# A four-layer cross-attention network in one core: norms loaded by broadcast, and the order of loads, tokens, divisions and stores changed at a dozen places

## The chip, the cores and the metric

The kernel runs on one core of one Trainium2 chip. Its time is the device time of one execution in microseconds (us). Three executions of the kernel before gave 1397.26, 1397.42 and 1398.39 us; the median, 1397.42, stands for it. The profile is of a further execution, which took 1396.16 us.

The core has five engines with queues of their own: TensorE (PE; the load of its stationary operand is shown as PEld), VectorE (DVE), ScalarE (ACT), GpSimd (POOL) and SyncE (SP, which here only issues DMAs).

## The reference

All numbers are float32. `x` has 4 batches of 256 tokens of 256 elements; `ctx` has 4 batches of 512 rows of 128. Four times a layer norm, a cross-attention and a residual sum follow each other, and then a layer norm, a feed-forward block and a residual sum:

```
# attention 0: 16 heads of 16; q and k are normed per head; the last 16 rows of
# ctx have their own k, v, norm weights and softmax, whose result is added
q = ln(x @ Wq + bq, qn); k = ln(y_main @ Wk + bk, kn); k_dca = ln(y_dca @ Wkv_dca + b, knd)
ctx = attn(q, k, v) + attn(q, k_dca, v_dca);  return ctx @ Wo + bo
# feed-forward 0: of 64 low-rank maps the 4 with the longest A x are taken
# attentions 1, 2, 3: 16 heads of 128, 8 key heads, mask, no bias
scores = (x @ Wq) (ctx @ Wk)^T / sqrt(128);  return softmax(scores) (ctx @ Wv) @ Wo
# feed-forward 1: 8 experts, 2 for each token, and a shared expert
# feed-forward 2: the one of 2 experts (gelu or relu) that a gate prefers
# feed-forward 3: the 64 tokens of each batch that a router scores highest
```

## The kernel before

The function that runs (`bounded_path`) holds one long program whose order is written out by hand for PE, ACT, DVE and POOL; each engine works through its own instructions in that order and waits on semaphores of others. A second path for inputs outside some bounds lies behind a branch and does not run. All is in tiles of 128 partitions; a batch of `x` is one tile `x_sb[b]` of 128 x 2 x 256, where partition p holds tokens 2p and 2p+1.

**Opening and layer 0** (to about 222 us). `Norm(b)` (L908 on) computes mean and reciprocal deviation of a batch, its `tokens` the normed tokens `xn`, and `layernorm_T` (L932) turns them into `xnT` by PE. The opening fills PE with matmuls nobody reads (`warm`, L1428). Weights are centred per head on DVE (`centred`, L1146). The norms' weights and biases, three loads `prm` of one partition each (L1061), are copied out on POOL into `rep`, and eight matmuls of one column (`pcols`) turn them into per-partition columns `cols`, which scale the turned queries and keys. `project_q`, `project_k`, `project_v` make queries, keys and values; class `Scale` makes the heads' reciprocal deviations in steps: `square` on ACT, `sum` on DVE, `power` on ACT, `root` (three DVE operations, L1247 to L1249) and `scaled` (L1252), whose result `pad` PE turns (`pT`, L1329) into qT (L1336) and kT (L1347, L1352). Scores are `ps` (L1361), the attended values `po` (L1371). In the loop over steps of batch b, the norm and the tokens of a later batch are placed at fixed steps i. Feed-forward 0 (`ysf`, L1497; added to x on POOL, L1498) ends with the tokens of layer 1's first batch.

PSUM: until the end of layer 0 banks come from a pool `ring`; then it is closed and a pool `psum` opened (L1750).

**Layers 1 to 3** (`attention`, L1777). Beforehand the query and key weights of a head are multiplied into one matrix (`folding`, L975: `pm` L986 into `m_sb`, `pn` L1002 into `n_sb`) from raw weights that `load_raw` (L958) brings from HBM, 1280 KB for each of four parts. Then come, for each of 32 pairs of a batch and two heads, queries, scores (`ps`, L1905), their exponential, and `po` (L1913). Sums are inverted and spread (`wide`, L1959, a DVE transpose), and the attended values are divided by a multiply of 128 x 512 (`divided`, L1960), on POOL and DVE in turn. The last four pairs are divided at the layer's end; `last_output` (`py`, L1995) then multiplies them by `n_sb`, first for token chunk 0, then 1, and `out.add` adds the other pairs' part `w` to x.

**Feed-forward 1** (552 to 655 us): lists of tokens by expert, indirect DMAs on POOL that fetch a block's tokens (`gather`, L2398), `turn_in` (pxg, L2406, and its copy xgT, L2408), expert matmuls (pgu, L2431) and the shared expert (`psh`, `pysh`, L2270).

**Feed-forward 2** (to about 1035 us): 9 blocks `blocks2`, of which blocks 0 to 4 hold the first three batches' tokens, and 5 to 8 the rest. Each has `gather` (L2795), `turn_in` (pxg, L2803; xgT, L2805), `weights` (a DVE copy `wa`, L2819, and an ACT copy `wb`), `rise2` (pb, L2833; z, L2838), `either` and `fall` (pyb, L2859; yb, L2863; a store `yd` on SP, L2864). Layer 3's four raw loads are issued on SP after the stores of blocks 0, 1, 4 and 5.

**Feed-forward 3** (to the end): `put` (L3235 to L3248) adds the routed tokens' part to x and stores a batch; batches 2 and 3 are computed in two column halves and stored whole, both by DMAs on ACT's queue.

```
for k in range(4):
    divided(B - 1, 4 + k, nc.vector if k % 2 else nc.gpsimd)     # layer's end
out.add()
...
(nc.scalar if i else nc.sync).dma_start(out[b]..., x_sb[b])      # put
```

## Time and profile before

| | us |
|---|---|
| median of three executions | 1397.42 |
| the profiled execution | 1396.16 |
| its span, first to last instruction | 1394.3 |
| outside the span | 1.86 |
| PE busy | 1377.1 |
| DVE busy | 887.7 |
| POOL busy | 682.8 |
| ACT busy | 580.3 |
| mean granted TensorE clock | 0.999 |

The page of the profile gives each engine's busy time with its share of the span and, as x and a number, its instructions; then the chain of work that ended last, followed back from the end, with its shares by engine; then groups of instructions by source line. The waits view lists, for one engine, who ended its idle times: the waiting tile and line, the releasing engine and tile, then us in all, the number of times and the longest. A timeline line gives start, length, engine, line, operation, output and inputs, shapes, and in brackets the idle time before it and who ended it. SPq and ACTq are DMAs as SP and ACT issue them: the time is that of the issue, not of the transfer. A matmul of float32 shows as two PE instructions (and PE's lines here name the number of these).

### The profile page before, as it was taken

The page shows a single profiled execution, that of the slowest core. Times are in us where ns is not written, and L with a number is a line of the kernel's source. Part 1 is how long each engine was busy: PE and PEld are TensorE (multiplying, and loading weights), DVE is VectorE, ACT ScalarE, POOL GpSimd, SP SyncE. Part 2 cuts the span into 40 slices and gives each one's busy share as a digit, 9 for nine tenths or more (in the row PEclk, how much of TensorE's full clock was granted, in tenths as well). Part 3 has the DMA queues.
Part 4 walks back from the last instruction along what each step waited for, and adds up shares of the span by engine and source line. Part 5 has one row for each costly group of instructions (what it writes and reads, how often), then busy time and mean ns, then how long its engine had stood idle before and what let it go on. Part 6 is the DMA issues. An engine that isn't in the chain of part 4 may idle for free.

```text
span 1394.3 us, 19995 instructions
## 1 busy us (share of the span) xinstructions
PE 1377.1 (99%) x7279; PEld 907.2 (65%) x7279; DVE 887.7 (64%) x2018; ACT 580.3 (42%) x1148; POOL 682.8 (49%) x822
## 2 busy tenths in 40 slices
PE   9999999999999999999999999999999999999998
PEld 7665676566656666887565666666875656666666
DVE  6667863665666547655576756549656758566675
ACT  5766454433344332256434333333264344333331
POOL 4223333466565455232577654566315775445560
PEclk9999999999999999999999999999999999999999
DMA  5000220300000001172110000000422000000000
GB/s 167 2 1 2 76 77 16 79 21 1 8 0 8 1 8 36 44 236 67 38 54 8 16 1 9 0 0 16 148 88 65 9 4 4 0 1 0 1 0 34
DMA packets 49622, 47.05 MB, mean 34 GB/s; under 512 B 8297, under 2 KB 45386, under 8 KB 49516
## 3 DMA queue, kind: packets, MB, share of 16 engines
q1 hardware_dynamic: 45868, 37.43, 8.9%
q0 software_dynamic: 2544, 6.95, 1.7%
q8 instruction: 60, 0.98, 0.3%
q10 hardware_dynamic: 1104, 1.31, 0.3%
q14 instruction: 46, 0.38, 0.1%
HBM read 38.73 MB, written 6.95 MB: 33 GB/s over the span
## 4 chain that ended last, share of the span: by engine, by line
PE 94%; DVE 2%; POOL 2%; DMA 1%; issue 1%; ACT 0%; SPq 0%; DVEq 0%; POOLq 0%
PE ps L1905 23%; PE po L1913 23%; PE paq L1875 6%; PE pao L1875 5%; PE pbq L1875 4%; PE pbo L1875 3%; PE ps L1361 2%; PE pyf L1495 2%; PE paf L1445 2%; PE pgu L2431 2%; PE po L1371 2%; PE psh L2253 1%; PE pm L986 1%; PE pn L1002 1%; PE py L1995 1%; PE pyb L2859 1%
## 5 line engine op out<-in xcount | busy, mean ns | idle before, releaser
L1924 POOL TENSOR_TENSOR half<-pT 128x1024 f32<-128x1024 f32 x93 | 218.4, 2348 | 288.9 <-ACT pT L1908 216.6
L1905 PE MATMUL ps<-qT,cT 128*128 128x512 f32 x768 | 345.6, 593 | 0.0
L1913 PE MATMUL po<-pT,c_sb 128*128 128x512 f32 x768 | 345.3, 592 | 0.0
L1908 ACT ACTIVATE pT<-ps,mbias 128x512 f32<-128x512 f32 x384 | 263.7, 687 | 155.4 <-PE ps L1905 139.8
L1913 PEld LDWEIGHTS po<-pT,c_sb 128*128 128x128 f32 x768 | 145.8, 190 | 183.2 <-issue 183.2
L1905 PEld LDWEIGHTS ps<-qT,cT 128*128 128x128 f32 x768 | 138.9, 190 | 138.4 <-issue 136.1
L1917 ACT COPY oT<-po 128x512 f32<-128x512 f32 x96 | 56.2, 586 | 265.2 <-PE po L1913 265.2
L1960 POOL TENSOR_TENSOR oT<-oT,wide 128x512 f32<-128x512 f32 x90 | 114.4, 1290 | 16.8 <-DVE wide L1959 16.8
L1885 DVE TENSOR_TENSOR qT<-qT,paq 128x128 f32<-128x128 f32 x90 | 25.5, 283 | 96.3 <-ACT qT L1884 96.3
L1365 ACT ACTIVATE pT<-ps 128x512 f32<-128x512 f32 x128 | 66.0, 602 | 26.5 <-PE ps L1361 26.2
L1932 DVE TENSOR_TENSOR half<-half 128x512 f32<-128x512 f32 x96 | 71.9, 749 | 2.7 <-POOL half L1922 2.5
L1934 DVE STREAM_TRANSPOSE turned<-half 128x512 f32<-128x512 f32 x96 | 68.3, 712 | 6.3
L1885 DVE TENSOR_TENSOR w<-w,pao 128x128 f32<-128x128 f32 x21 | 6.0, 286 | 103.0 <-ACT w L1884 103.0
L1875 PE MATMUL paq<-xnT_a,m_sb 128*128 128x128 f32 x360 | 71.3, 280 | 0.0
L1875 PE MATMUL paq<-xx,m_x 128*128 128x128 f32 x360 | 69.6, 275 | 0.0
L1875 PEld LDWEIGHTS paq<-xnT_a,m_sb 128*128 128x128 f32 x360 | 57.2, 192 | 16.7 <-issue 8.5
L1938 DVE TENSOR_REDUCE sums<-turned 128x16 f32<-128x512 f32 x96 | 65.8, 686 | 3.3
L1875 PE MATMUL pao<-n_x,ox 128*128 128x128 f32 x336 | 65.0, 275 | 0.0
L1884 ACT COPY qT<-paq 128x128 f32<-128x128 f32 x90 | 23.9, 265 | 94.1 <-PE paq L1875 94.1
L1959 DVE STREAM_TRANSPOSE wide<-rz 128x512 f32<-128x512 f32 x96 | 62.2, 686 | 0.1
L1888 DVE TENSOR_TENSOR qT<-qT,pbq 128x384 f32<-128x384 f32 x90 | 49.9, 554 | 9.7 <-DVE qT L1887 0.5
L1875 PEld LDWEIGHTS paq<-xx,m_x 128*128 128x128 f32 x360 | 54.7, 192 | 0.0
(484 smaller groups left out, 2530.2 us busy)
## 6 DMA issues: line engine op xcount, KB each, us to landing
wq<-in_L_wqT SPq DMA_DIRECT2D x11, 512.0 KB
wo<-in_L_wo SPq DMA_DIRECT2D x11, 512.0 KB
yd<-yr SPq DMA_DIRECT2D x20, 128.0 KB
xd<-xn_f SPq DMA_DIRECT2D x8, 256.0 KB
w<-in_F_w SPq DMA_DIRECT2D x4, 512.0 KB
wk<-in_L_wkT SPq DMA_DIRECT2D x11, 128.0 KB
wv<-in_L_wvT SPq DMA_DIRECT2D x11, 128.0 KB
yd<-yb SPq DMA_DIRECT2D x9, 128.0 KB
```

The source lines that it names most:

```text
L1365: nc.scalar.activation(pT[kp][:, j], ps[j], AF.Exp)
L1875: nc.tensor.matmul(p[:, at, :], lhsT=lhsT, rhs=rhs, start=(k == 0 and at == 0), stop=(k == len(of) - 1 and i == which[-1]),)
L1905: nc.tensor.matmul(ps, lhsT=cT[:, b, k * P : (k + 1) * P], rhs=qT, start=True, stop=True)
L1908: nc.scalar.activation(pT[:, k, :], ps, AF.Exp, bias=mbias[:, b, k : k + 1])
L1913: nc.tensor.matmul(po, lhsT=c_sb[:, b, k, :], rhs=pT[:, k], start=(k == 0), stop=(k == NK - 1))
L1917: done["head"] = nc.scalar.copy(raw, po).ins
L1924: nc.gpsimd.tensor_tensor(half, pT[:, 0:2], pT[:, 2:4], ALU.add)
L1932: nc.vector.tensor_tensor(part, half[:, 0], half[:, 1], ALU.add)
L1934: nc.vector.transpose(turned.rearrange("p f i -> p (f i)"), part)
L1938: nc.vector.tensor_reduce(sums[b, hp // 4][:, hp % 4, :], turned, AX.X, ALU.add)
L1959: nc.vector.transpose(wide, rzs[b, hp // 4][:, hp % 4, :, None].to_broadcast([P, NB, 32]))
L1960: eng.tensor_tensor(outs[b, hp], outs[b, hp], wide.rearrange("p f i -> p (f i)"), ALU.mult)
```

## The change

- Norms: `prm` is loaded onto all 128 partitions; on each, the elements of its own lane are picked by a product with `lane0` (made from the identity) and a sum. The copies `rep` on POOL and the eight `pcols` matmuls are gone; `columns_of_norms` moves ahead of add_q. One `warm` group is 3 in place of 4; the first queries go ahead of the biases on PE; the centring of `wq0` goes ahead of that of the bias rows; the first heads' `root` is made by four POOL operations; ACT's copies of the values of batch 0 for the last rows come after qT and kT.
- In batch 1 of layer 0 the norm of batch 3 and its tokens are placed one step later; the tokens of layer 1's first batch go before the last output step of feed-forward 0.
- The pool of banks is changed after layer 1's first queries.
- The last division of layers 1 to 3 is done by halves (128 x 256): first the four first halves (for token chunk 0), then the second.
- Feed-forward 1: block 0's `turn_in` goes ahead of the second `pysh` of batch 2; the first `pysh` of batch 3 goes ahead of `pm`.
- Feed-forward 2: raw loads 1, 2, 3 of layer 3 are issued after the stores of blocks 4, 5 and 6 (before: 1, 4 and 5); block 6's weights are copied before block 4's `fall`.
- The stores of batches 2 and 3 go by column halves, batch 3's on SP and batch 2's on ACT.

The diff, cut to its core (line numbers of before in the headers):

```diff
@@ 1052 @@ opening: loads, lanes, columns
-        rep = w0.tile([1, 8, 4, 2, HD0], F32, tag="qT0", name="rep")
-        prm = l0.tile([1, 3, 2, HD0], F32, tag="prm", name="prm")
+        prm = l0.tile([P, 3, 2, HD0], F32, tag="prm", name="prm")
...
-            nc.sync.dma_start(prm[:, i], t[f"L0_{n}"].rearrange("(o a) x -> o a x", o=1))
+            nc.sync.dma_start(prm[:, i], t[f"L0_{n}"].partition_broadcast(P))
...
-        nc.vector.memset(rep, 0.0)
+        nc.vector.tensor_reduce(
+            lane0.rearrange("p o x -> p (o x)"), ident.rearrange("p (a q) -> p q a", q=2 * HD0), AX.X, ALU.add
+        )
+        nc.vector.tensor_reduce(halves0, lane0, AX.X, ALU.add)
+        nc.vector.tensor_tensor(lane0[:, 0], lane0[:, 0], lane0[:, 1], ALU.add)
...
+            def root_aside(self, a, z):
+                v, r, e = (t[:, a:z] for t in (self.v, self.r, self.e))
+                nc.gpsimd.tensor_tensor(e, r, r, ALU.mult)
+                nc.gpsimd.tensor_tensor(e, e, v, ALU.mult)
+                nc.gpsimd.tensor_scalar(e, e, -0.5, 1.5, ALU.mult, ALU.add)
+                nc.gpsimd.tensor_tensor(r, r, e, ALU.mult)
...
         def columns_of_norms():
-            pn = state0.pop()
-            c_v = cols.rearrange("p i a -> p (i a)")
-            nc.vector.tensor_scalar(c_v[:, :4], pn[:, :4], HD0 ** -0.5, None, ALU.mult)
-            nc.vector.tensor_copy(c_v[:, 4:], pn[:, 4:])
+            nc.vector.tensor_tensor(by_lane, prm, lane0[:, 0, None, None, :].to_broadcast(wide), ALU.mult)
+            nc.vector.tensor_reduce(pairs, by_lane, AX.X, ALU.add)
+            for o in range(2):
+                nc.vector.tensor_scalar(
+                    cols[:, o, :], pairs[:, 0, :], halves0[:, o : o + 1], HD0 ** -0.5, ALU.mult, ALU.mult
+                )
+            nc.vector.tensor_copy(cols[:, 2:, :], pairs[:, 1:, :])
@@ 1509 @@ opening: order
+        centred(by_head(wq0), by_head(wq0), mq)
         centred(by_head(crow), by_head(crow), head_sums(by_head(crow), 3), 3)
-        centred(by_head(wq0), by_head(wq0), mq)
...
-        warm(4)
+        columns_of_norms()
+        warm(3)
+        add_q = project_q(0)
         spread_biases()
-        add_q = project_q(0)
         add_q()
...
-        context_T(1)
-        norm_columns()
         sc0.sum(0, NC)
...
         sc0.square(True, NC + 2, NQK)
+        context_T(1)
         sc0.sum(NC, NC + 2)
+        ones_of_values()
+        sc0.root_aside(0, NC)
+        last_context(1)
...
-        sc0.root(0, NC)
         sc0.scaled(0, NC)
@@ 1615 @@ layer 0
-                if i == 5:
+                if i == (5 if n == 1 else 6):
                     norms[n + 1] = Norm(n + 1, f"a0_{n + 1}")
-                elif i == 6:
+                elif i == (6 if n == 1 else 7):
                     xns[n + 1] = norms[n + 1].tokens()
...
+                if n == 6:
+                    xn1 = norm.tokens()
                 if n:
                     arrows[n].output()
@@ 1751, 2008 @@ pool of banks
-    del banks["ring"]
-    banks["psum"] = ctx.enter_context(tc.tile_pool(name="psum", bufs=2, space=PSUM))
...
             first_queries(0)
+            if "ring" in banks:
+                del banks["ring"]
+                ring.close()
+                banks["psum"] = ctx.enter_context(tc.tile_pool(name="psum", bufs=2, space=PSUM))
@@ 2054 @@ layers' ends
+            widths = []
+            for k in range(0, 4, 2):
...
+                for j in range(2):
...
+                    nc.vector.transpose(wide, rzs[B - 1, 1][:, k + j, :, None].to_broadcast([P, NB, 32]))
...
+                divided_half(k, widths[k], 0, nc.gpsimd)
+                divided_half(k + 1, widths[k + 1], 0, nc.vector)
             for k in range(4):
-                divided(B - 1, 4 + k, nc.vector if k % 2 else nc.gpsimd)
+                divided_half(k, widths[k], 1, nc.vector if k % 2 else nc.gpsimd)
             out.add()
@@ 2524, 2563 @@ feed-forward 1
+            blocks[0].turn_in()
             shared[2].down(1)
             shared[2].add(1)
-            for j in range(-2, NBLK + 1):
+            for j in range(-1, NBLK + 1):
...
+            shared[3].down(0)
             for n in range(N8):
                 next(fold)
                 if n < NC:
-                    shared[3].down(n)
+                    if n:
+                        shared[3].down(n)
@@ 2976 @@ feed-forward 2
-            load_raw(3, 1, done["slots2"])
...
             blocks2[6].turn_in()
+            blocks2[6].weights(fp)
             blocks2[4].fall(fp)
-            load_raw(3, 2, done["slots2"])
+            load_raw(3, 1, done["slots2"])
...
                     rise2(5)
-                    blocks2[6].weights(fp)
...
                 blocks2[i].fall(fp)
+                if i in (5, 6):
+                    load_raw(3, i - 3, done["slots2"])
                 if i == 5:
-                    load_raw(3, 3, done["slots2"])
@@ 3248 @@ stores
-                (nc.scalar if i else nc.sync).dma_start(out[b].rearrange("(p c) d -> p c d", c=NC), x_sb[b])
+                (nc.scalar if i and not b % 2 else nc.sync).dma_start(
+                    out[b].rearrange("(p c) d -> p c d", c=NC)[:, :, cols], x_sb[b][:, :, cols]
+                )
...
-        put(1, cols=a, store=False)
+        put(1, cols=a)
```

More of the change, by code (lines that the diff above doesn't have):

```diff
@@ L848, in bounded_path @@
     w0 = first.enter_context(tc.tile_pool(name="w0", bufs=2, side="right"))
-    banks = {"ring": first.enter_context(tc.tile_pool(name="ring", bufs=6, space=PSUM))}
+    ring = ctx.enter_context(ExitStack())
+    banks = {"ring": ring.enter_context(tc.tile_pool(name="ring", bufs=6, space=PSUM))}
     def bank(tag, shape, name):
@@ L1103, in bounded_path @@
         nc.gpsimd.memset(c_last, 0.0)
-        nc.vector.memset(rep, 0.0)
+        lane0 = l0.tile([P, 2, HD0], F32, tag="lane0", name="lane0")
+        halves0 = l0.tile([P, 2], F32, tag="halves0", name="halves0")
+        nc.vector.tensor_reduce(
[3 more added lines that the diff above has]
+        nc.vector.tensor_tensor(lane0[:, 0], lane0[:, 0], lane0[:, 1], ALU.add)
         rows = l0.tile([P, 2], F32, tag="rows", name="rows")
@@ L1201, in project_k, with project_v @@
             return lambda: nc.vector.tensor_tensor(qks[b][:, NC + k0 : NC + k0 + 2, :], pk, bias, ALU.add)
-        def project_v(b):
+        def project_v(b, later=None):
             for k0 in range(0, NK + 1, 2):
@@ L1209, in project_v, with kept @@
                     nc.tensor.matmul(pv[:, k - k0], lhsT=ck, rhs=wvo[:, int(k == NK)], start=True, stop=True)
-                for o, (h, _) in enumerate(halves):
-                    if k0 < NK:
-                        nc.scalar.copy(vals[b % 2][:, k0 : k0 + 2, o, :, h], pv[:, :, o])
-                    else:
-                        nc.scalar.copy(vals_d[b % 2][:, o, :, h], pv[:, 0, o])
+                def kept(k0=k0, pv=pv):
+                    for o, (h, _) in enumerate(halves):
+                        if k0 < NK:
+                            nc.scalar.copy(vals[b % 2][:, k0 : k0 + 2, o, :, h], pv[:, :, o])
+                        else:
+                            nc.scalar.copy(vals_d[b % 2][:, o, :, h], pv[:, 0, o])
+                if later is None:
+                    kept()
+                else:
+                    later.append(kept)
         class Scale:
@@ L1258, in bounded_path, with columns_of_norms @@
         cols = l0.tile([P, 4, 2], F32, tag="cols", name="cols")
-        state0 = []
-        def norm_columns():
-            pn = bank("o", [P, 8], "pcols")
-            for i in range(8):
-                nc.tensor.matmul(
-                    pn[:, i : i + 1],
-                    lhsT=rep[:, i].rearrange("o h i x -> o (h i x)"),
-                    rhs=ident[:1, :1],
-                    start=True,
-                    stop=True,
-                )
-            state0.append(pn)
-        def columns_of_norms():
-            pn = state0.pop()
-            c_v = cols.rearrange("p i a -> p (i a)")
-            nc.vector.tensor_scalar(c_v[:, :4], pn[:, :4], HD0 ** -0.5, None, ALU.mult)
-            nc.vector.tensor_copy(c_v[:, 4:], pn[:, 4:])
+        def columns_of_norms():
+            wide = [P, 3, 2, HD0]
+            by_lane = l0.tile(wide, F32, tag="by_lane", name="by_lane")
+            pairs = l0.tile([P, 3, 2], F32, tag="pairs", name="pairs")
+            nc.vector.tensor_tensor(by_lane, prm, lane0[:, 0, None, None, :].to_broadcast(wide), ALU.mult)
[3 more added lines that the diff above has]
+                    cols[:, o, :], pairs[:, 0, :], halves0[:, o : o + 1], HD0 ** -0.5, ALU.mult, ALU.mult
+                )
+            nc.vector.tensor_copy(cols[:, 2:, :], pairs[:, 1:, :])
         def score_bound():
-            nc.vector.tensor_tensor(prm, prm, prm, ALU.mult)
+            row = prm[:1]
+            nc.vector.tensor_tensor(row, row, row, ALU.mult)
             wmx = l0.tile([1, 3], F32, tag="wmx", name="wmx")
-            nc.vector.tensor_reduce(wmx, prm[:, :, 0, :], AX.X, ALU.max)
+            nc.vector.tensor_reduce(wmx, row[:, :, 0, :], AX.X, ALU.max)
             bsm = l0.tile([1, 3], F32, tag="bsm", name="bsm")
-            nc.vector.tensor_reduce(bsm, prm[:, :, 1, :], AX.X, ALU.add)
+            nc.vector.tensor_reduce(bsm, row[:, :, 1, :], AX.X, ALU.add)
             nc.vector.scalar_tensor_tensor(wmx, wmx, float(HD0), bsm, ALU.mult, ALU.add)
@@ L1516, in bounded_path @@
                 nc.gpsimd.tensor_copy(wvo[:, n, o].rearrange("p (q j) x -> p q j x", q=2), wv[:, o])
-        for o in range(2):
-            nc.gpsimd.tensor_copy(rep[:, 2 * o : 2 * o + 2, :, o, :], prm[:, 0, :, None, :].to_broadcast([1, 2, 4, HD0]))
-        nc.gpsimd.tensor_copy(
-            rep[:, 4:].rearrange("o i h a x -> o i (h a) x"),
-            prm[:, 1:].rearrange("o i a x -> o (i a) x")[:, :, None, :].to_broadcast([1, 4, 8, HD0]),
-        )
-        warm(4)
+        columns_of_norms()
+        warm(3)
+        add_q = project_q(0)
         spread_biases()
-        add_q = project_q(0)
         add_q()
@@ L1537, in bounded_path @@
         sc0.square(True, NC + 2, NQK)
+        context_T(1)
         sc0.sum(NC, NC + 2)
+        ones_of_values()
+        sc0.root_aside(0, NC)
+        last_context(1)
         sc0.sum(NC + 2, NQK)
         sc0.power(NC, NQK)
-        project_v(0)
-        ones_of_values()
-        last_context(1)
-        columns_of_norms()
-        sc0.root(0, NC)
+        kept = []
+        project_v(0, kept)
+        for one in kept[:2]:
+            one()
         sc0.scaled(0, NC)
@@ L1553, in bounded_path @@
         transposed(0, 4)
+        kept[2]()
         norm = Norm(1, "a0_1")
@@ L1734, in bounded_path @@
                 norm = Norm(0, "a1_0")
-            if n == 6:
-                xn1 = norm.tokens()
             if n == 0:
@@ L1960, in divided, with divided_half @@
                 eng.tensor_tensor(outs[b, hp], outs[b, hp], wide.rearrange("p f i -> p (f i)"), ALU.mult)
+            def divided_half(k, wide, c, eng):
+                o = outs[B - 1, 4 + k].rearrange("p (h c s) -> p c h s", h=2, c=NC)
+                eng.tensor_tensor(o[:, c], o[:, c], wide[:, c], ALU.mult)
             def o_sums(b, hp, eng):
@@ L2053, in attention @@
             out.products(lambda: quotients(B - 1, 1))
+            widths = []
+            for k in range(0, 4, 2):
+                if k:
+                    pair = ap.tile([P, 2, NB, 32], F32, tag="half", name=f"wide{L}", bufs=1 if L == 1 else 2)
+                for j in range(2):
+                    if k:
+                        wide = pair[:, j]
+                    else:
+                        wide = ap.tile([P, NB, 32], F32, tag="turned", name=f"wide{L}_{j}")
+                    nc.vector.transpose(wide, rzs[B - 1, 1][:, k + j, :, None].to_broadcast([P, NB, 32]))
+                    widths.append(wide.rearrange("p f i -> p (f i)").rearrange("p (h c s) -> p c h s", h=2, c=NC))
+                divided_half(k, widths[k], 0, nc.gpsimd)
+                divided_half(k + 1, widths[k + 1], 0, nc.vector)
             for k in range(4):
-                divided(B - 1, 4 + k, nc.vector if k % 2 else nc.gpsimd)
+                divided_half(k, widths[k], 1, nc.vector if k % 2 else nc.gpsimd)
             out.add()
```

## The prediction

> **What bounds the kernel now.** I read the page's busy times first, then the chain of waits that ended last, then TensorE's waits by releaser, and last the timeline around the longest of them.

> ```profile
> span 1394.3 us, 19995 instructions
> ...
> PE 1377.1 (99%) x7279; PEld 907.2 (65%) x7279; DVE 887.7 (64%) x2018; ACT 580.3 (42%) x1148; POOL 682.8 (49%) x822
> ...
> PE 94%; DVE 2%; POOL 2%; DMA 1%; issue 1%; ACT 0%; SPq 0%; DVEq 0%; POOLq 0%
> ```

> TensorE (PE) is busy for 1377.1 of 1394.3 us, and 94% of the chain that ended last lies on it. So the kernel is as long as TensorE's work plus TensorE's idle time, 17.2 us, and a change that leaves the bulk of the matmuls alone can gain some part of those 17 us and no more. The next view says for whom PE waits (us in all, times, longest).

> ```profile
> PE pxg L2803 <- DMA xg<-xd,who_2l: 1.6, 1, 1.6
> PE pwarm L1428 <- POOL ident masks.py:199: 1.5, 1, 1.5
> PE py L1995 <- POOL oT L1960: 1.5, 4, 0.5
> PE pb L2833 <- DVE wa L2819: 1.3, 1, 1.3
> PE pT L1329 <- DVE pad L1252: 0.7, 1, 0.7
> PE pT L1329 <- DVE qT L1336: 0.7, 1, 0.7
> PE pgu L2431 <- ACT xgT L2408: 0.7, 2, 0.4
> PE pxn_a L938 <- DVE xn_a L926: 0.6, 2, 0.4
> PE pq L1857 <- DVE ysf L1497: 0.6, 1, 0.6
> PE pm L986 <- ACT yr L2460: 0.6, 1, 0.6
> PE ppick L3203 <- DVE xgT L3171: 0.4, 1, 0.4
> PE py L3242 <- DVE blk L3233: 0.4, 1, 0.4
> PE ps L1361 <- ACT kT L1352: 0.3, 1, 0.3
> ```

> These 13 rows sum to 10.9 us. The change touches the places behind all of them but pwarm, ppick, the last py (L3242) and one of the two pgu waits. The program orders of both kernels, laid side by side, show that PE's instructions and waits in the attention of layers 1 to 3 stay as they are but for each layer's last output and the first queries of layer 1; that is the body of the 94%. Below I price a wait by the gap that it leaves in PE's start-to-start times beyond the usual spacing (the waits view counts a little less).

> **The change, part by part** (minus is a gain).

> 1. Opening, −1.1. Before: pbias 8.46, pq 9.91, add_q on DVE at 12.02, the first norm's root (three operations, 17.02 to 17.65) in DVE's chain, pad 17.69, kT on ScalarE to 21.36, first ps 21.41. After: pq comes right behind the xnT copy (it ends at 8.21), so it runs 8.26 to 10.0; pbias 10.0 to 11.1, its copy to 11.7, add_q 11.75: 0.27 earlier. The root goes to POOL, beside DVE's sums; POOL's small operations take 0.18 to 0.28 us (L1123, L1131), so four take about 1.0 against 0.63 on DVE, but DVE's own chain loses them and the two column copies (0.15 each). DVE then reaches pad at 16.45 in place of 17.69, and ps starts near 20.03 in place of 21.41. The five operations on columns that come in their stead (one of 128x96, four small, about 1.0 us by L1237's 0.18 and L1236's 0.67 for 512) lie ahead of add_q, where DVE sat idle for 1.57. The eight pcols matmuls (1.9 us of PE) lay before PE's waits here, not on the chain. Some of the 1.38 is lost again where the next tokens are awaited (pxn_a at 25.0, by my chain 23.9). Bounds: −0.3 (only add_q's start) to −1.4.
> The three loads of norms now fill 128 rows; before they were issued at 4.84 to 6.26 and are needed at about 10. The nearest row of 128 rows is an issue of about 0.42 (x_sb, c_sb) against 0.21 to 0.25, so SP's later loads come 0.6 later; c_sb for context 1 is used at 13.7, so nothing waits.

> 2. Batch 1 of layer 0: Norm(3) goes behind the second qT. PE's 1.07 gap at 76.54 (pT waits for qT) goes. The norm's five small operations (73.99 to 75.77) now delay what follows on DVE, and the transposes of xn_a0_3 and the copy y_sb come later; I give back half: −0.5, bounds −0.3 to −1.0.

> 3. Tokens of layer 1's first batch one step earlier: gaps of 0.29 and 0.40 at 215.3 and 215.95 go, xn_a is then ready long before: −0.7.

> 4. The pool of banks is opened after the first queries. The 0.77 at 223.07 (pq for ysf) goes. But the second pq now takes a bank of the ring that the copy of the first qT frees: pq 1.8 us, then ScalarE's copy, 0.59 (L1862), and two hand-overs, before the second pq may start; a wait of about 0.85 takes the old one's place. +0.1, bounds −0.1 to +0.3. The copy is queued on ScalarE behind nothing; behind the waiting pq stand the first scores.

> 5. Last division by halves. End of layer 1: gaps 0.42 and 0.68 (544.5, 547.0). The 512-wide multiply takes 1.26 on POOL and on DVE beside it; the 256-wide one 0.72 on POOL (L1498) and 0.42 on DVE alone (L2002). The first halves are ready some 0.55 earlier, which covers the first gap, and of the second pair POOL's is ready at about 545.8 and DVE's at 546.3, where PE asks at 546.1 and 547.1: −1.1. DVE does the same work in more instructions, so the w additions start up to 0.2 later; they have 0.7 before x_sb needs py, and the next product waits 2.1 us of psh. Layer 2: −0.7 (977.4). Layer 3: −0.3 (1361.9).

> 6. Block 0 of F1 turned in before pysh: its gather was issued at 577.28, pxg starts at 584.67, so it is there; the 0.40 at 585.52 goes. −0.4.

> 7. pysh3_0 ahead of pm: 0.62 at 637.61 stays. Both need a bank that ScalarE's yr frees; the wait passes to pysh. 0, bounds 0 to +0.2.

> 8. Loads of layer 3 moved behind the rest blocks. This is the largest, so its lines (start, length, engine, line, instruction, wait):

> ```profile
> 994.04 0.37 SPq L970 DMA_DIRECT2D wq<-in_L_wqT  x1
> ...
> 998.12 1.02 POOL L2795 DMA_INDIRECT xg<-xd,who_2l  x1 [10.97 <-DVE where L2761]
> ...
> 1003.76 0.87 PE L2803 MATMUL pxg<-ident,xg 128*128 128x128 f32 x4 [1.63 <-DMA xg<-xd,who_2l]
> ...
> 1008.79 0.69 DVE L2819 COPY wa<-w2a 128x1028 f32 x1
> ...
> 1009.62 2.02 PE L2833 MATMUL pb<-xgT,wa 128*128 128x128 f32 x16 [1.26 <-DVE wa L2819]
> ```

> ```profile
> 993.50:1001.00 7.50, 7.50 (x55) 7.09 (x53) 4.06 (x19) 2.14 (x4) 2.27 (x3) 1.00 1.06 339
> ```

> In the second fence (busy times of PE, PEld, DVE, ACT, POOL, then clock, DMA share, GB/s) the 16 DMA engines are full from 993.5 to 1001: two raw loads of 1280 KB. The gather issued at 998.12 moves its first packet at 1001.10, when they are through, and PE, free at 1002.13, gets it at 1003.76: a gap of 1.79. An earlier gather, with no load about (issued 967.95), moved its first packet after 1.75 and was through after 2.46. Without load (3,1) the queues are empty by about 998, and the gather lands at 998.12 + 2.46 = 1000.6, before PE asks. −1.6. The loads that go later: each is 4.3 us of transfer at the rate above; (3,1) is issued at about 1006 and lands by 1012, needed at 1019; (3,2) lands by 1020, needed at 1025; (3,3) by 1024, needed at 1028.6. The smallest cover is 4.6 us.
> [...]

> 9. blocks2[6].weights earlier. pb at 1009.62 waited 1.42 for wa (0.69), queued on DVE behind z (1008.18). After, wa is copied at about 1003.2, where DVE idles (3.35 before yb at 1006.40); the wait that comes last is then PE's own work. −1.3, with 0.1 for what DVE's yb loses.

> 10. Last stores by halves. Before: ScalarE issues two stores of 256 KB at 1389.09 and 1389.60; their packets (2 KB, 88 ns) run from 1389.95 to 1391.76 and the last lands at 1392.18. After, half the bytes are gone by then, and SP takes one of the two. A 512-byte packet takes 27 ns in wk's loads, so 256 of them on 16 engines take 0.43 per store in place of 0.70; started at 1389.60 + 0.86 the last ends at about 1391.0 and lands at 1391.4. −0.7, bounds 0 (if the pieces cost more) to −0.9.

> **Sum.** 1.1 + 0.5 + 0.7 − 0.1 + 1.1 + 0.7 + 0.3 + 0.4 + 0 + 1.6 + 1.3 + 0.7 = 8.3. The profiled execution took 1396.16 (span 1394.3 and 1.86 around it): 1387.9. It lies 1.26 below the median of the runs shown, 1397.42, so the median after is forecast at **1389.1**.

> **Rivals.**
> A. The gather shares the DMA engines with the loads as they run, and is late by something of its own (its descriptors, or the write of xd before it). For: three gathers follow each other in 2.6 us, and their 96 packets end only at 1003.93. Against: 1.75 us after its issue it was due at 999.87, and nothing of it moved until 1001.10. The 1.6 stays: 1390.7. [...] Chance 0.08.
> B. DVE takes the waits' place at the layers' ends and in the opening: its work there is no less (four transposes of 0.67 and the multiplies, 5.1 us before and after), and POOL beside it slows it (1.26 against 0.69 for 512 columns alone). The 2.1 of part 5 and 0.8 of part 1 come back: 1392.0. With A: 1393.6. Chance 0.17.
> C. The change does not do what it says: each closed wait opens elsewhere, as in part 4, and less than 2.8 is left: 1394.6 to 1397.4. For: parts 4 and 7 do just that. Against: the slack worked out for parts 5, 8 and 9. Chance 0.08.
> D. Slower: the granted TensorE clock falls, since the last idle moments go. Place: the attention of layers 1 to 3, at 99% busy. Price: 1% of 1377.1 is 13.8 us. It eats the whole gain from 8.3/1377.1 = 0.6% down, a clock of 0.993 in place of the 0.999 measured; at 0.99 the time is 1389.1 + 12.4 = 1401.5. Against: PE was already busy 99% at 0.999, and the clock only fell to 0.50 after the last matmul, when PE idled. [...] Chance 0.04.

> **How the numbers follow.** Forecast 0.63 (1387 to 1390.5), A 0.08, B 0.17, C 0.08, D 0.04. With every part at its better bound the gain is 9.9, or 1387.5; runs spread by some tenths below: low end 1386.5. The upper end reaches past B with A: 1394. About 0.2% (2.8 us) is what a measurement of this kernel can tell from no change: faster (under 1394.6) 0.86, the same 0.09 (C and the edge of B), slower 0.05.

> **What would show it.** In the profile after, PE's waits for xg (L2803's place), wa, oT, the qT of batch 1 and ysf should be gone, and a wait of pq for ScalarE's qT should stand near 223. The first ps should start near 20.0, the gather of block 5 land before PE is free, and the last store's packets end 0.7 earlier. I am wrong if pm of layer 3 waits for wq, if new DVE waits stand at the layers' ends, or if the clock is under 0.995.

## The result and the profile after

Six executions of the changed kernel took 1388.31 to 1391.00 us, median **1389.21**; six of the kernel before beside them had a median of 1397.57. The ratio is 0.994, with a 95% interval of 0.9929 to 0.995. The profiled execution took 1389.42 us with a span of 1387.6.

The page of the profile after (span, busy times, chain by engine):

```profile
span 1387.6 us, 19978 instructions
...
PE 1374.4 (99%) x7261; PEld 906.5 (65%) x7261; DVE 886.8 (64%) x2026; ACT 580.8 (42%) x1148; POOL 684.8 (49%) x829
...
PE 94%; POOL 2%; DVE 2%; DMA 1%; issue 1%; ACT 0%; DVEq 0%; ACTq 0%; POOLq 0%
```

The span is 6.7 shorter. PE's busy time fell by 2.7 and its idle time from 17.2 to 13.2. TensorE's waits by releaser in the profile after:

```profile
PE pT L1341 <- DVE pad L1271: 2.3, 2, 1.4
PE pwarm L1440 <- POOL ident masks.py:199: 1.5, 1, 1.5
PE pxg L2834 <- DVE n_sb L1006: 0.7, 1, 0.7
PE pq L1864 <- ACT qT L1869: 0.7, 1, 0.7
PE pysh L2298 <- ACT yr L2488: 0.6, 1, 0.6
PE pb L2864 <- DVE wa L2850: 0.5, 1, 0.5
PE ppick L3234 <- DVE xgT L3202: 0.4, 1, 0.4
PE py L3273 <- DVE blk L3264: 0.4, 1, 0.4
PE pgu L2459 <- ACT xgT L2436: 0.3, 1, 0.3
PE pxn_a L939 <- DVE xn_a L927: 0.2, 1, 0.2
```

Gone are the waits for the gather (1.6), for oT (1.5), for ysf and for the pT of batch 1; the wait for wa is 0.5 in place of 1.3, and another block's. New are pq for qT (forecast) and pxg for n_sb (not forecast), and the first row grew from 0.7 to 2.3. A ledger says what each place is worth: for every PE instruction that both kernels have, its start after minus its start before, from the two profiled executions; a step in this shift is time won or lost there. A closed wait wins a little more than its gap: the second matmul behind it follows 0.22 us after the first, where behind the wait it was 0.32 (`py` at 544.52 before); this 0.10 is counted with the wait.

| part | forecast | ledger |
|---|---|---|
| 1 opening (to 25 us) | −1.1 | **+0.40** |
| 2 norm of batch 3 | −0.5 | −0.46 |
| 3 tokens of layer 1 | −0.7 | −0.76 |
| 4 pool of banks | +0.1 | +0.08 |
| 5 ends of layers 1, 2, 3 | −1.1, −0.7, −0.3 | −1.31, −0.89, −0.43 |
| 6 feed-forward 1, block 0 | −0.4 | −0.87 |
| 7 pysh ahead of pm | 0 | +0.09 |
| 8 loads and gather | −1.6 | −1.12 |
| 9 wa earlier | −1.3 | −1.02 |
| 10 stores | −0.7 | −0.45 |
| sum | −8.3 | −6.74 |

Parts 2, 3, 4 and 7 came out within 0.1, and part 5 gave 0.5 more than forecast. The opening had the wrong sign. The sum is that of the two profiled executions, 6.74; the medians moved by 8.36.

**The opening.** Timeline of the profile after (start, length, engine, line, instruction, wait before it):

```profile
6.32 0.33 SPq L1061 DMA_DIRECT2D prm<-in_L_knd  x1
...
11.82 0.26 DVE L1283 TENSOR_TENSOR by_lane<-prm,lane 128x96 f32<-128x96 f32 x1 [2.13 <-DMA prm<-in_L_knd]
...
12.74 0.69 DVE L1191 TENSOR_TENSOR qk<-pq,bqk 128x512 f32<-128x512 f32 x1
```

The third load of norms, issued at 6.32, released DVE only at 11.82; the same load on one partition, issued at 6.26 in the kernel before, had landed at 7.13. On 128 partitions each load is 128 pieces of 128 bytes; the 384 pieces start at 6.26 and the last sixteen not before 10.57. So add_q, forecast at 11.75, ran at 12.74. A second thing stands in the windows of 2 us (busy us of PE, PEld, DVE, ACT, POOL with their instructions, then the granted clock, DMA share, GB/s):

```profile
16.00:18.00 2.00, 0.59 (x3) 0.21 (x2) 1.91 (x6) 1.42 (x5) 1.06 (x5) 1.00 0.24 63
18.00:20.00 2.00, 1.13 (x7) 0.93 (x8) 1.90 (x6) 1.61 (x5) 0.00 (x0) 0.83 0.60 87
20.00:22.00 2.00, 1.98 (x11) 1.55 (x13) 1.20 (x2) 1.10 (x3) 0.00 (x0) 0.50 0.80 292
22.00:24.00 2.00, 2.00 (x20) 1.47 (x13) 1.78 (x7) 0.76 (x2) 0.00 (x1) 0.81 0.99 369
```

The clock fell to half: (1 − 0.83)/0.5 × 2 + 2 + (1 − 0.81)/0.5 × 2 = 3.44 us of it by the windows, 3.41 by the switches that the trace records (19.33 and 22.74), with eight head transposes in that stretch. In the kernel before it was 1.00 here. The two idle times just ahead are 1.42 and 0.86 us, and TensorE was busy for 1.30 of the 3.41 us ahead of the fall (15.92 to 19.33).

### The profile page after: what moved, and what is told of

Read it like the earlier page. It is cut to its first block, busy times and chain, and to the rows that moved or that the text cites. A ratio compares the mean times of both kernels' runs of the same rounds, so it can differ in the third digit from the quotient of the medians.

```text
span 1387.6 us, 19978 instructions
## 1 busy us (share of the span) xinstructions
PE 1374.4 (99%) x7261; PEld 906.5 (65%) x7261; DVE 886.8 (64%) x2026; ACT 580.8 (42%) x1148; POOL 684.8 (49%) x829
## 3 DMA queue, kind: packets, MB, share of 16 engines
q10 hardware_dynamic: 1360, 1.05, 0.2%
## 4 chain that ended last, share of the span: by engine, by line
PE 94%; POOL 2%; DVE 2%; DMA 1%; issue 1%; ACT 0%; DVEq 0%; ACTq 0%; POOLq 0%
PE ps L1912 23%; PE po L1920 23%; PE paq L1882 6%; PE pao L1882 5%; PE pbq L1882 4%; PE pbo L1882 4%; PE ps L1373 3%; PE po L1383 2%; PE paf L1457 2%; PE pyf L1507 2%; PE pgu L2459 2%; PE psh L2281 1%; PE py L2006 1%; PE pm L987 1%; PE pn L1003 1%
## 5 line engine op out<-in xcount | busy, mean ns | idle before, releaser
L1967 POOL TENSOR_TENSOR oT<-oT,wide 128x512 f32<-128x512 f32 x84 | 106.8, 1292 | 0.0
L1966 DVE STREAM_TRANSPOSE wide<-rz 128x512 f32<-128x512 f32 x84 | 54.4, 685 | 0.0
```

The lines of the kernel that those rows point to most:

```text
L1966: nc.vector.transpose(wide, rzs[b, hp // 4][:, hp % 4, :, None].to_broadcast([P, NB, 32]))
L1967: eng.tensor_tensor(outs[b, hp], outs[b, hp], wide.rearrange("p f i -> p (f i)"), ALU.mult)
```

## The experiments

Each is the changed kernel with the edit shown, unless it says otherwise. The first four shared a chip (kernel before there: 1397.22), the next four another (1397.81), the last four a third (1397.80).

**The changed kernel again**, x0_after, no edit.

> The changed kernel itself, measured beside the next three on one chip. Theory and rival: the same as before, about 1389.2 us, some 8.4 under the kernel before; in the opening the first ps again near 21.4 and the first pxn_a of batch 1 near 25.4.

Measured: 1389.75 (1388.79 to 1393.49), ratio 0.9955 [0.9941, 0.9969]. The half clock at 18 to 24 us was there again (0.79, 0.50, 0.86). Its runs are wide: 1393.49 with a mean clock of 0.995, 1388.79 with 1.000.

**The opening of before**, x1_opening_before: part 1 undone, the rest kept.

```diff
-            nc.sync.dma_start(prm[:, i], t[f"L0_{n}"].partition_broadcast(P))
+            nc.sync.dma_start(prm[:, i], t[f"L0_{n}"].rearrange("(o a) x -> o a x", o=1))
...
-        sc0.root_aside(0, NC)
+        sc0.root(0, NC)
```

> The changed kernel with its whole opening put back (loads of one row, the rep copies and the eight column matmuls, root on DVE, the old order). Theory (the new opening gains nothing: the norms' loads land late, and TensorE's clock halves in the gap that the removed matmuls leave): pxn_a of batch 1 back at 25.0 in place of 25.4, no half clock between 18 and 24, so 0.3 to 0.4 us faster than the changed kernel. Rival (the opening gains the 1.1 us forecast, and the loss lies elsewhere): 1.1 slower than the changed kernel.

Measured: 1392.27 (1391.55 to 1392.77), ratio 0.9964 [0.9951, 0.9978]. At the opening the clock was whole and the ledger against the changed kernel read −0.26: the old opening is no worse than the new one as profiled. The 3 us of loss in this profile lie where this edit touches nothing, in feed-forward 1:

```profile
572.00:574.00 2.00, 1.97 (x15) 1.85 (x14) 1.32 (x7) 0.00 (x0) 0.00 (x0) 0.79 0.00 0
574.00:576.00 2.00, 2.00 (x6) 1.69 (x7) 1.22 (x8) 0.00 (x0) 0.43 (x1) 0.50 0.00 0
576.00:578.00 2.00, 2.00 (x6) 1.60 (x5) 0.75 (x2) 0.00 (x0) 1.70 (x2) 0.50 0.20 55
578.00:580.00 2.00, 2.00 (x6) 1.44 (x6) 0.30 (x1) 0.00 (x0) 1.39 (x3) 0.50 0.28 84
580.00:582.00 2.00, 2.00 (x11) 1.60 (x10) 0.67 (x2) 0.34 (x1) 0.53 (x1) 1.00 0.43 123
```

PE is busy for all but 0.03 us here, yet the clock is half for 0.84 + 6 = 6.84 us, twice 3.42, and twelve pysh records take 5.47 us in place of 2.8. Just before (569.80 to 574.40) stand the list matmuls `plist`: 16 matmuls (32 records) of 40 columns, which go at the pace of VectorE's `at`: in the profile after the 32 records take 4.08 us, and `at` comes in four groups of four, 1.11 or 1.12 us from one group's start to the next. The profiles of before, of the changed kernel and of x0 have 1.00 here.

**Idle matmuls in the opening**, x2_fill.

```diff
+        warm(6)
         sc0.scaled(0, NC)
         second = transposed(0, 0, True)
...
+        warm(3)
         sc0.scaled(NC, NC + 2)
```

> The changed kernel with matmuls that nobody reads in TensorE's two gaps of the opening: six behind pv, three behind the first pT. Theory (the half clock comes from TensorE's idle time of 1.4 and 0.9 us there): granted clock 1.00 from 18 to 24 us, the eight later pT matmuls in about 1.1 in place of 1.94, pxn_a of batch 1 near 24.4 in place of 25.4, 1.0 us faster than the changed kernel. Rival (the chain through DVE and ScalarE sets these times, the clock is of no consequence): pxn_a stays at 25.4 and the time with it.

Measured: 1389.79 (1388.40 to 1392.73), ratio 0.9951 [0.9938, 0.9965]. The clock at the opening was whole and the ledger there −0.82, but 1.7 went again at 572 to 578 (clock 0.83, 0.50, 0.82), and the median is that of x0: the 1.0 us expected does not show. Nor are the −0.82 the fillers' for sure: three later profiles with the opening of the changed kernel, unfilled (x5, x6, x7), had the whole clock too, at −1.04, −0.39 and −0.79. So the half clock at the opening comes in some executions and not in others, and x2 does not show that the fillers prevent it.

**Norms loaded ahead of the bias rows**, x3_prm_early.

```diff
+        for i, n in enumerate(("qn", "kn", "knd")):
+            nc.sync.dma_start(prm[:, i], t[f"L0_{n}"].partition_broadcast(P))
         nc.sync.dma_start(crow[0:1, 0, :], t["L0_bq"].partition_broadcast(1))
```

> The changed kernel with the three loads of norms issued ahead of the bias rows on SP. Theory (by_lane waited until 11.8 for the last of these loads, so add_q came at 12.74 and not at 11.75): by_lane near 10, add_q near 11.75, the first pad near 16.4 in place of 17.2, the first pxn_a of batch 1 0.8 or more earlier, as TensorE's gap is shorter too; 0.8 to 1.5 us faster. Rival (the loads of one row for 128 partitions are slow in themselves, some 3.6 us for the last, and hold up whatever stands behind them in SP's queue): the bias rows come late in their place, add_q no earlier, no gain.

Measured: 1388.66 (1388.31 to 1391.42), ratio 0.9939 [0.9925, 0.9952]. by_lane ran at 10.64, add_q at 11.84, and the ledger at 25.4 read −1.61 with a whole clock; the profiled execution (1391.42) then lost 3.3 in feed-forward 1 (0.89, three times 0.50, 0.90). The loads are as slow as the rival says (issued at 1.72 to 2.70, last piece at 7.73), but ahead of the bias rows that is early enough.

**The loads of layer 3 as before**, x5_loads_before.

```diff
-            load_raw(3, 1, done["slots2"])
+            load_raw(3, 2, done["slots2"])
...
-                if i in (5, 6):
-                    load_raw(3, i - 3, done["slots2"])
                 if i == 5:
+                    load_raw(3, 3, done["slots2"])
```
(and load 1 back behind the store of block 1)

> The changed kernel, with the loads of the rest blocks' weights back in the order of before (the third load again ahead of the gather that it delays). Theory of the prediction: the gather for block 6 again stands behind a running load on the same 16 DMA engines and its transposes start 1.2 us later than in the changed kernel (what the ledger of start times gave for this step), so about 1389.4 + 1.2 = 1390.6. Rival A (the gather is late for its own reason): the order changes nothing, under 0.3 us, 1389.4.

Measured: 1389.43 (1389.15 to 1389.75), ratio 0.9941 [0.9925, 0.9956]. By the median that is rival A; the trace says otherwise. The two timelines, the changed kernel first, then x5:

```profile
994.40 1.02 POOL L2826 DMA_INDIRECT xg<-xd,who_2l  x1 [10.97 <-DVE where L2792]
...
998.65 0.68 DVE L1006 COPY n_sb<-pn 128x512 f32<-128x512 f32 x1
...
999.31 0.70 DVE L2850 COPY wa<-w2a 128x1028 f32 x1
...
999.39 0.44 PE L2834 MATMUL pxg<-ident,xg 128*128 128x128 f32 x2 [0.75 <-DVE n_sb L1006]
```

```profile
993.49 1.02 POOL L2826 DMA_INDIRECT xg<-xd,who_2l  x1 [10.97 <-DVE where L2792]
...
997.74 0.68 DVE L1006 COPY n_sb<-pn 128x512 f32<-128x512 f32 x1
...
998.75 0.87 PE L2834 MATMUL pxg<-ident,xg 128*128 128x128 f32 x4 [1.24 <-DMA xg<-xd,who_2l]
```

With the loads back, the DMA engines are full until 996.5 (a share of 1.05 from 989) and the gather issued at 993.49 moves its first packet at 996.55, 3.06 us later; in the changed kernel it takes 1.74 (994.40 to 996.14). The wait of 1.24 for the gather is back (+1.33 in the ledger), but the wait for n_sb that stands in its shadow is gone (−0.67). So the order of loads is worth 0.66 net, not 1.2, and the place and the wait are the forecast's. The profiled execution hides it because its opening ran at the whole clock and was 1.04 ahead; the clocks of the other three (0.999 and 1.000) fit the same reading, but their openings were not traced.

**The division by whole heads**, x6_whole_division.

```diff
-                divided_half(k, widths[k], 1, nc.vector if k % 2 else nc.gpsimd)
+                divided(B - 1, 4 + k, nc.vector if k % 2 else nc.gpsimd)
```
(and the first halves with their transposes taken out)

> The changed kernel, with the last division of each layer by whole heads again. Theory: the waits at the ends of layers 1, 2 and 3 come back with the 1.1 + 0.7 + 0.3 us that the ledger gave for them, 1389.4 + 2.1 = 1391.5. Rival C (waits that reopen take the gain): under 0.7 us. Feed-forward 1 is reached 1.1 us later than in the changed kernel, so whether its list matmuls fall into a stretch of half clock is decided anew; that could add up to 3.3 us and is read from the clock row, apart from the ledger of the layer ends.

Measured: 1392.54 (1391.60 to 1394.33), ratio 0.996 [0.9945, 0.9975]. The row of before is back to the digit:

```profile
PE py L2002 <- POOL oT L1967: 1.5, 4, 0.5
```

The ledger against the changed kernel gives 1.31, 0.89 and 0.43 at the three ends, 2.63 in all, just what the changed kernel won there and 0.5 more than the 2.1 expected. The rest of the difference between the two profiles is 1.7 of half clock in feed-forward 1 (0.75, 0.50, 0.90: 3.4 us of it), 0.6 behind it and 0.3 at the gather. By the median, 1392.54, the 1391.5 expected is passed by 1.0.

**Block 6's turn-in later**, x7_turn6.

```diff
-            blocks2[6].turn_in()
             blocks2[6].weights(fp)
             blocks2[4].fall(fp)
+            blocks2[6].turn_in()
```

> The changed kernel, with the turn-in of block 6 put behind the downward matmuls of block 4 instead of ahead of them. Theory: the 0.75 us for which the transposes of block 6 wait for VectorE's n_sb copy (queued behind the wa copy) is covered by those matmuls, so -0.7, 1388.7. Rival: block 6's weights or its upward matmuls become late by the same amount, no change.

Measured: 1387.85 (1387.62 to 1389.36), ratio 0.9932 [0.9917, 0.9947]. The wait for n_sb is gone, and the ledger falls from −0.79 to −1.93 at 999.66: 1.1 gained, of which 0.2 is given back at the next pb (1001.39); the 0.96 that stays is more than the wait's 0.75.

**Wide list matmuls**, x10_wide: x3 with `plist` 120 columns wide; the 80 added columns are thrown away.

```diff
-                bring = tile8("bring", [P, 2, N8, 2, NBLK])
+                bring = tile8("bring", [P, 2, N8 + 2, 2, NBLK])
+                nc.gpsimd.memset(bring[:, :, N8:], 0.0)
...
-                        state["plist"], lhsT=at, rhs=state["bring"][:, i, c], start=(n == 0), stop=(n == 2 * N8 - 1)
+                        state["plist"], lhsT=at, rhs=state["bring"][:, i, c : c + 3], start=(n == 0), stop=(n == 2 * N8 - 1)
```

> The kernel of x3 (norms' loads ahead of the bias rows), with the 32 list matmuls of feed-forward 1 made 120 columns wide instead of 40 (the added 80 columns are thrown away; they change no output). Theory: the half-clock stretch that x3 showed at 570 to 580 us comes because TensorE, though counted as busy, moves few columns while it goes through the list matmuls at VectorE's pace (127 ns each); with three times the columns at the same pace the clock stays at 1.00 there and about 3.3 us of x3's profiled 1389.6 + 0.5 go, so about 1386.5 in a profile and at most 1388.7 (x3's median) over all runs. Rival 1: the stretch comes from too much work, not too little: it stays or grows, 1388.7 or more. Rival 2: the wider matmuls outlast VectorE's pace and cost up to 32 x 80 ns = 2.6 us themselves, which eats the gain.

Measured: 1388.00, all five runs within 1387.53 to 1388.39, ratio 0.993 [0.9916, 0.9943]; the profile (1387.83) has 1.00 throughout. The 32 records take 4.14 us against 4.08: the added columns cost nothing. The 1386.5 expected for the profile took x3's span, 1389.6, for its time; from the 1391.42 of that execution 3.3 less is 1388.1. But x3 had its stretch for sure in one run of five alone, the profiled one (the other four 1388.31 to 1389.22), so the next pair decides.

**The same on x1**, x13_opening_before_wide. x1's five runs all lay above 1391.5 with a clock of 0.997 or 0.998.

> x1 (the opening of before in the changed kernel) with the list matmuls of feed-forward 1 made 120 columns wide (80 of them thrown away). All five runs of x1 lay at 1391.6 to 1392.8 with a granted clock of 0.997 or 0.998, and its profile had 3.3 us of half clock at 572 to 580 us. Theory (thin matmuls at VectorE's pace let the clock fall there): the stretch goes in nearly every run, the clock reads 0.999 or 1.000, and the time falls by 2.5 to 3.3 us to 1389 to 1389.8. Rival 1 (the stretch hangs on when feed-forward 1 is reached, not on the columns moved): the median stays within 1 us of 1392.3. Rival 2 (the wide matmuls are slower than VectorE): under 1 us is gained although the clock is whole.

Measured: 1389.56 (1389.01 to 1390.64, six runs, each with a clock of 0.999), ratio 0.9937 [0.9921, 0.9954]. Its slowest run is faster than x1's fastest; 2.7 are gained. The two were not measured on the same chip, so the profiles are the better witness: from one to the other PE's starts move by −3.32 between 574 and 580. The windows of x1 shown above now read:

```profile
572.00:574.00 2.00, 2.00 (x18) 1.83 (x17) 1.34 (x7) 0.00 (x0) 0.00 (x0) 1.00 0.00 0
574.00:576.00 2.00, 2.00 (x11) 1.76 (x10) 1.90 (x10) 0.00 (x0) 1.27 (x2) 1.00 0.00 0
576.00:578.00 2.00, 2.00 (x11) 1.54 (x10) 0.68 (x2) 0.00 (x0) 1.70 (x2) 1.00 0.41 111
578.00:580.00 2.00, 2.00 (x11) 1.76 (x10) 0.91 (x2) 0.38 (x1) 1.07 (x2) 1.00 0.26 86
580.00:582.00 2.00, 2.00 (x12) 1.72 (x11) 1.29 (x3) 0.76 (x2) 0.24 (x1) 1.00 0.22 66
```

Same PE busy time, same pace of VectorE, three times the columns: the clock stays whole, and PE runs eleven records of 256 columns in 2 us where it ran six.

**Where the clock halves.** Windows of 2 us blur it; the switches of the clock that each trace records settle it. In all 14 profiles they lie whole multiples of 3.413 us apart (13.65, 3.41 and 1361.92 us in the changed kernel are 4, 1 and 399 times that, 1385.81 us in the kernel before 406 times), and the clock first rises 4.62 to 7.50 us after the first instruction. Lines laid every 3.413 us from these switches, called the grid here, cut an execution into pieces. The table shows where the list matmuls start against the nearest line of the grid, how many columns TensorE's records move in the poorest piece of the grid there, and the clock in the next piece. The median piece moves 4025 in the profiles of before and of the changed kernel; a record that crosses a line is counted by its share of time.

| profile | list columns | start after a grid line, us | columns in the piece | clock in the next |
|---|---|---|---|---|
| x2 | 40 | −0.67 | 1117 | 0.50 |
| x6 | 40 | −0.61 | 1103 | 0.50 |
| x1 | 40 | +0.04 | 1194 | 0.50, twice |
| x3 | 40 | +0.29 | 1403 | 0.50, twice |
| before | 40 | +0.68 | 1787 | 1.00 |
| x7 | 40 | +0.73 | 1815 | 1.00 |
| x5 | 40 | +0.84 | 1904 | 1.00 |
| changed kernel | 40 | +1.11 | 2133 | 1.00 |
| x0 | 40 | +1.24 | 2243 | 1.00 |
| x10 | 120 | −0.59 | 3226 | 1.00 |
| x13 | 120 | +0.20 | 3288 | 1.00 |

So in the four profiles where the narrow lists (4.1 us long at whole clock) start from −0.67 to +0.29 and leave a piece of 1403 columns or fewer, the clock halved; in the five from +0.68 to +1.24, with 1787 or more, it stayed whole. Rival 1 of x13 is half right: with 40 columns the clock goes with the place on the grid in these nine. But x10 and x13 start at −0.59 and +0.20, where with the narrow lists the clock halved, and stay whole with 3226 and 3288 columns (x11, x12 and x14 lie elsewhere on the grid and show nothing here). The opening fits: the clock halved after pieces of 1205 and 1418 columns (the changed kernel and x0), and in no other profile, where the poorest piece after the first rise had 1612 or more. The kernel's last piece stands outside this count: there the clock halved after 1808 columns (x14), part of them in matmuls of 64 rows; nothing was run on this.

**The same on the kernel before**, x14_before_wide.

> The kernel before with nothing changed but the list matmuls' width, 120 columns instead of 40. Its runs spread with their clocks: those at 0.999 lie near 1396.5 to 1397, those at 0.997 near 1398 to 1400, and the one profiled at 1396.16 had the clock whole at feed-forward 1. Theory: part of the 1.26 us between that profile and the median is such stretches, so the median falls by 0.7 to 1.3 us to 1396.2 to 1396.9, with fewer runs over 1398. Rival: the spread comes from elsewhere and the median stays at 1397.4 within 0.3.

Measured: 1396.81 over 12 runs beside 1397.80 over 17 of the kernel before, ratio 0.9991 [0.9981, 1.0001]. A mean clock of 0.997 or less was read in 6 of the 17 and in none of the 12. The move is the size that was expected, but its interval just takes in no change.

**All three edits**, x11_best (x3, x7 and the wide lists together) and x12_best_fill (with `warm(3)` at x2's two places besides).

> Three edits together on the changed kernel: the norms' loads ahead of the bias rows (x3: 1.75 us at the opening in its ledger, of which 0.8 to 1.2 belong to runs of the changed kernel with a half clock there), block 6's turn-in behind block 4's downward matmuls (x7: 1.1), and the wide list matmuls (x10). x10 was 1388.0 with the first and the last; with 1.1 less, 1386.9, and all runs within 1 us of each other. Rival (the gains overlap, since an earlier opening only moves the wait of block 6): 1387.5 or more.

> x11 with two groups of three idle matmuls in the opening, behind pv and behind the first head's transposes of batch 0, where TensorE waited 0.9 and 0.5 us. Theory: they keep the clock whole there in every run, and take no time of their own: x11's time or 0.3 less, with the slowest runs nearer the median. Rival: with the early norms' loads the gaps are already too short for the clock to fall, and the added matmuls delay the transposes behind them: 0.2 to 0.6 us slower than x11.

Measured: x11 1387.23 (1386.79 to 1388.53), ratio 0.9922 [0.9905, 0.9938]; x12 1387.34 (1386.42 to 1388.29), ratio 0.9921 [0.9905, 0.9937]. Both lie 2 us below the median of the changed kernel. In x12 PE's idle time at 16 to 20 us shrank from 1.48 to 0.19, but the clock was whole in both: the fillers gain and cost nothing that shows. x11 came 0.3 above its expectation and under its rival's bound; its runs spread over 1.7 us, not the 1 expected.

## Why the prediction was right, and where it was not

**Bound and sum.** That the kernel is PE's work and PE's waits, and that this change can only close waits, holds in the main: of the 6.74 us, 4.0 are idle time of PE. The other 2.7 are busy time, which the prediction's bound of 17 us leaves out: the pcols matmuls were 1.9 of it, and py, the layers' last product, takes 1.2 less, while the half clock in the opening gives some back. The forecast for the profiled execution was 1387.9, and it took 1389.42; that the median came to 1389.21, by the forecast's 1389.1, is partly luck. The prediction carried over the 1.26 us by which the median of before lay above its profile. The median of after lies 0.21 below its own. Two slips in the working change nothing: the better bounds given add up to 9.5, not 9.9, and a raw load of 1280 KB at the rate shown takes 3.9 us, not 4.3. x14 says what part of the 1.26 probably was: stretches of half clock in feed-forward 1, which some runs of before have and its profiled one had not.

**Part 1** failed: −1.1 forecast, +0.40 measured. Two steps of it did. "The three loads of norms now fill 128 rows ... needed at about 10": priced by the issue on SP (0.42 against 0.21) and not by the landing, 5.5 us after the issue. Loaded earlier, the opening gives −1.21, −1.01, −0.85 and −0.78 against before (x3, x10, x11, x12: the ledger at 25.4 plus 0.40), about what was forecast; loaded as written but with the whole clock it gives −0.64, +0.01 and −0.39 (x5, x6, x7). So the late landing costs about 0.6. And "The eight pcols matmuls (1.9 us of PE) lay before PE's waits here, not on the chain": with them gone PE idled for 1.42 and 0.86, and in the profiled execution the clock fell; against the mean of the three that is about 0.7. They moved one column each, but behind them pv started at 16.30, nearer to the head transposes than the 14.27 of the changed kernel. That removing the matmuls is what lets it fall was not tried by itself.

**Parts 2, 3, 4 and 7** were right to 0.1, with the waits where they were forecast: pq for qT at 224.03, pysh in pm's place. **Part 5** gave 2.63 for 2.1, and x6 shows that the halves are worth it: the 0.5 more is 0.10 at each of five places, which the gap alone leaves out.

**Part 6** was too small. The turn-in gave −0.50 at 585.5 for −0.4; another 0.37 came by 623, where ScalarE's yr copies wait for the stores of yd, which now fall otherwise (waits of 1.48 and 0.29 us before, 0.22 and 1.31 after). Nothing was run on this.

**Part 8** had the mechanism right (first packet 1.74 us after the gather's issue in the changed kernel, 3.06 with the loads back in x5) and missed what is late next: block 6's transposes need a bank that the copy n_sb frees. That copy reads pn, which ends at 998.42, and stands behind block 5's wa copy (998.05) on VectorE, as it did before; so it ends at 999.33. The copy that part 9 moved, block 6's, comes only behind it (999.31) and is not the cause. In the kernel before, n_sb was through at 1003.05 and the gather at 1003.72, so the later wait hid it. x7 gets the time back by letting block 4's downward matmuls run meanwhile.

**Part 9**: the wait of 1.42 went in full (−1.39), and 0.37 of it came back at 1013, where the next block's pb waits 0.46 for its own wa.

**Part 10**: −0.45 for −0.7, within its bounds.

**Rivals.** A falls by x5: the gather starts as the loads run out (its first packet at 996.55, the loads' last at 997.8), and not before. Until 996.5 the loads had the 16 engines full (a share of 1.05). B falls by the layers' ends, where no DVE wait appeared. C happened in small: n_sb, wa and qT took 0.7, 0.5 and 0.7 us. D named the wrong place and the wrong mechanism, but the clock did cost something: not 1% everywhere, but whole stretches of 3.4 us at half.

**Still open**: what sets the place of the grid in an execution. The profiles show it for one execution of each kernel. By the mean clocks x1 fell into the stretch at feed-forward 1 in all five runs and x5 in none (0.999 or 1.000), and the changed kernel in some, though the three reach it within about 1 us of each other. By an estimate from the table, places spread evenly would let such lists fall in about a third of the runs (−0.67 to +0.29 and somewhat beyond, of 3.41); five of five does not look like that. Nothing was run on this.

## What to carry to other kernels

Price a load by when its last piece lands, not by its issue, above all when one short row is spread over 128 partitions (here 0.33 us of issue and 5.5 us until VectorE was released). When the wait that ends last is closed, look up what ends next to last: here a bank's release, hidden by 0.67 us. Before the medians of two kernels are compared, look at the granted clock in short windows and not at its mean: 3.4 us at half clock lower the mean by 0.001 and cost 1.7 us, more than most parts of this change. Here the place was behind a stretch of thin matmuls that waits on another engine: 32 records of 40 columns in 4.08 us, and behind them 6.83 us of half clock in x1.
